# Macaron block: the hidden planes stored with the columns of the four token tiles by turns

## Chip, cores and metric

The kernel runs on one core of one Trainium2 chip. The metric is device time in microseconds of one execution, the median of several runs.

## The reference

What is computed is a block of two feed-forward layers with an attention layer between them, for 16 sequences of 512 tokens with 256 features:

```python
x = x + 0.5 * ffn(layernorm(x), w_gate, w_up, w_down)
x = x + attn(layernorm(x), wq, bq, wk, bk, wv, bv)      # one head of 256, rotary q and k
x = x + 0.5 * ffn(layernorm(x), w_gate, w_up, w_down)

def ffn(x, w_gate, w_up, w_down):                       # weights: int in -127..127, times 1/127
    gate, up = x @ wg.T, x @ wu.T                       # 256 -> 768
    return (silu(gate) * up) @ wd.T                     # 768 -> 256
```

## The kernel before, in words

The work is cut into 48 stages: 16 sequences through the first feed-forward, the 16 through attention, the 16 through the second feed-forward. Each stage holds one sequence, four tiles of 128 tokens. Stages overlap: layer statistics, normalization and the transposition of a later stage are issued between the steps of the current one, in an order written out by hand (`steady`, `opening`, and the main loops). There is no scheduler that would reorder it; each engine's queue is worked in the order of issue.

A feed-forward stage (`ffn`) takes six steps, one for each 128 of the 768 hidden features. One step `h` is:

- `products` (L339): eight matmuls of 512 columns. The stationary tile is a 128x128 piece of the gate or up weights, the moving operand is the stage's transposed, normalized input. That input is held as two planes, zT_h (rounded to float32r) and zT_l (the rest), which are multiplied one after the other and summed in PSUM. Within a plane the even and the odd columns lie apart, 1024 bytes from each other, and `some_columns` reads them by turns.
- `hidden`: ACT takes silu of the gate (L351, act), DVE multiplies with up (L353), into PSUM, tile "tr".
- `beside(h)`: pieces of other stages, of which zT_h (L217, on ACT) and zT_l (L222, on POOL) split the next stage's input into its planes.
- `hidden_planes`: through `planes`, ACT casts the product from PSUM to float32r, hT_h (L217), and DVE subtracts it from the product to get the rest, hT_l (L222). Both write a [128, 512] SBUF tile in the order token tile c, block a, column j, so that the 128 columns of token tile c lie side by side.
- `down` (L316): eight matmuls of 256 columns. For each plane and each token tile c the stationary tile is the 128x128 piece of hT_h or hT_l, the moving operand the down weights of this step, whose even and odd columns also lie 1024 bytes apart and are read by turns. They accumulate over the six steps in PSUM. After the sixth, `finish` (L289, DVE) adds them to x.

`down` is held back: step h's down projection is issued after the products of step h+2 (`LAG = 2`, the list `behind`). The last step of the last stage is done in two halves of two token tiles each (256 columns), so that its end comes sooner.

TensorE's weight load is an instruction of its own in the profile (PEld), one ahead of each matmul. Float32 matmuls of attention (L555, L586, L606, L625) show as two records each. Weights come in by DMA as integers and are cast on POOL in the prologue. A second, plain version of all layers stands behind a condition that the inputs of this reference don't meet.

Of the kernel before, what the change touches and what calls it, by code (L numbers as in the profile page):

```python
# [17 lines left out]
P = 128  # L18
Q = 32
NQ = P // Q  # L20
# [15 lines left out]
def macaron_kernel(ctx: ExitStack, tc: tile.TileContext, x, wq, wk, wv, bq, bk, bv, wg, wu, wd, cos, sin, out):  # L36
# [134 lines left out]
    def layers(exact, work, att):  # L171
# [35 lines left out]
        def planes(sources, pool, shape, name, bufs, engine, seen):  # L207


            if not exact:  # L210
                whole = pool.tile(shape, F32, name=f"{name}_w", tag=f"{name}_h", bufs=bufs)
                for n, source in enumerate(sources):
                    nc.scalar.copy(seen(whole, n), source)
                return [whole], lambda: None
            high = pool.tile(shape, F32R, name=f"{name}_h", tag=f"{name}_h", bufs=bufs)
            for n, source in enumerate(sources):
                nc.scalar.copy(seen(high, n), source)  # L217
            low = pool.tile(shape, F32R, name=f"{name}_l", tag=f"{name}_l", bufs=bufs)

            def rest():  # L220
                for n, source in enumerate(sources):
                    engine.tensor_tensor(seen(low, n), source, seen(high.bitcast(F32), n), ALU.subtract)  # L222

            return [high, low], rest
# [50 lines left out]
        def some_columns(t, tiles):  # L275

            some = slice(tiles.start * Q // 2, tiles.stop * Q // 2)
            return t.rearrange("p e (a f) -> p a f e", a=NQ)[:, :, some, :]

        def down_weights(h):  # L280

            if exact:
                return wf["d"][:, h // 2, :, h % 2, :].rearrange("p e f -> p f e")
            return wf["d"][:, h, :]

        def finish(i, half, acc, last):
            _, b = stages[i]
            x_half = xs[b][:, 2 * half : 2 * half + 2, :]
            nc.vector.scalar_tensor_tensor(x_half, acc, DOWN, x_half, ALU.mult, ALU.add)  # L289
            if last:  # L290
                queue = nc.scalar if i == len(stages) - 1 else nc.sync
                queue.dma_start(
                    out=out[b].rearrange("(p c) d -> p c d", c=NC)[:, 2 * half : 2 * half + 2, :], in_=x_half
                )
# [3 lines left out]
        def down_step(n):  # L298
            while len(behind) > n:
                behind.pop(0)()  # L300

        def ffn(i, last, beside):
            zT = ready.pop(i)
            accs = []

            def down(h, halves):

                if not accs:
                    accs.extend(ps_acc.tile([P, 2, D], F32, name="acc") for _ in range(NC // 2))


                for tiles_of in [range(NC)] if h < NH - 1 else [(0, 1), (2, 3)]:
                    for n in range(len(halves[0])):
                        for c in tiles_of:
                            t = halves[c // 2][n]
                            nc.tensor.matmul(  # L316
                                accs[c // 2][:, c % 2, :],
                                t[:, bass.ts(c % (t.shape[1] // P), P)],
                                down_weights(h),
                                start=h == 0 and n == 0 and c % 2 == 0,  # L320
                                stop=h == NH - 1 and n == len(halves[0]) - 1,
                                skip_group_check=True,
                            )
                    if h == NH - 1:
                        half = tiles_of[0] // 2
                        finish(i, half, accs[half], last)

            def products(hs, columns=slice(0, NC)):

                nt = columns.stop - columns.start  # L330
                pairs = [[ps_mm.tile([P, nt * P], F32, name="mm", tag="mm") for _ in "gu"] for _ in hs]
                if len(hs) > 1:

                    turns = [(0, 0, 0), (0, 0, 1), (0, 1, 0), (1, 0, 0), (1, 0, 1), (0, 1, 1), (1, 1, 0), (1, 1, 1)]
                    turns = [(turn, w) for turn in turns for w in range(2)]
                else:
                    turns = [((n, 0, k), w) for n in range(len(zT)) for w in range(2) for k in range(KD)]
                for (n, h, k), w in turns:
                    nc.tensor.matmul(  # L339
                        pairs[h][w],  # L340
                        wf["gu"[w]][:, k, bass.ts(hs[h], P)],
                        some_columns(zT[n][:, k], columns),
                        start=n == 0 and k == 0,
                        stop=n == len(zT) - 1 and k == KD - 1,
                    )
                return dict(zip(hs, pairs))

            def hidden(gate, up):

                act = work.tile(list(gate.shape), F32, name="act", tag="rope", bufs=6 if exact else 4)  # L350
                nc.scalar.activation(act, gate, AF.Silu, scale=WSCALE)  # L351
                hid = ps_tr.tile(list(gate.shape), F32, name="tr", tag="tr")
                nc.vector.tensor_tensor(hid, act, up, ALU.mult)  # L353
                return hid

            def hidden_planes(hid):
                tiles, rest = planes(
                    [hid.rearrange("p (a c j) -> p c a j", a=NQ, j=Q)],
                    work,
                    list(hid.shape),  # L360
                    "hT",
                    5,
                    nc.vector,
                    lambda t, _: t.rearrange("p (c a j) -> p c a j", a=NQ, j=Q),
                )
                rest()
                return tiles

            found = {}
            for h in range(NH):  # L370
                if last and i == len(stages) - 1 and h == NH - 1:
                    halves = [
                        hidden_planes(hidden(*products([h], slice(c, c + 2))[h])) for c in (0, 2)
                    ]
                    down_step(0)
                    down(h, halves)
                    break
                if h not in found:
                    found.update(products([0, 1] if exact and i == 0 and h == 0 else [h]))
                hid = hidden(*found.pop(h))  # L380
                down_step(LAG - 1)
                beside(h)
                tiles = hidden_planes(hid)
                behind.append(lambda h=h, tiles=tiles: down(h, [tiles] * 2))
                beside(h + 0.5)
# [268 lines left out]
        for b in range(B):  # L654
# [13 lines left out]
            if b + 1 < B:  # L668
                rotated = queries_keys(i + 1)

                def beside(a):
                    if a == 0:
                        measure(i + 3, (0, 1))
                    elif a == 2:
                        measure(i + 3, (2, 3))
# [75 lines left out]
```

## Time and profile before

| what | value |
|---|---|
| median of 3 runs | 907.65 us (907.25 to 908.27) |
| profiled execution, its own time | 907.49 us |
| its span, first to last instruction | 905.6 us |
| granted TensorE clock | 1.00 |
| matmuls of L316 | 1536, at a mean of 275 ns in the record |
| their weight loads | 1536, at a mean of 191 to 192 ns |
| hT_h on ACT, 512 columns | 191, mean 583 ns |
| hT_l on DVE, 512 columns | 191, mean 676 ns |

How to read the profile: a line gives engine, operation, what is written and from what, shapes, count, busy time and mean length. PE rows are matmuls, PEld rows weight loads. A matmul's record includes the way through the array, so records overlap: a record of 275 ns doesn't mean that 275 ns pass until the next one starts. For TensorE's pace one reads the starts. The chain of waits follows the work that ended last back in time; the table of stretches gives each engine's busy time in a part of the span.

### The profile page before, as it was taken

The page shows a single profiled execution, that of the slowest core. Times are in us where ns is not written, and L with a number is a line of the kernel's source. Part 1 is how long each engine was busy: PE and PEld are TensorE (multiplying, and loading weights), DVE is VectorE, ACT ScalarE, POOL GpSimd, SP SyncE. Part 2 cuts the span into 40 slices and gives each one's busy share as a digit, 9 for nine tenths or more (in the row PEclk, how much of TensorE's full clock was granted, in tenths as well). Part 3 has the DMA queues.
Part 4 walks back from the last instruction along what each step waited for, and adds up shares of the span by engine and source line. Part 5 has one row for each costly group of instructions (what it writes and reads, how often), then busy time and mean ns, then how long its engine had stood idle before and what let it go on. Part 6 is the DMA issues. An engine that isn't in the chain of part 4 may idle for free.

```text
span 905.6 us, 12799 instructions
## 1 busy us (share of the span) xinstructions
PE 897.8 (99%) x4392; PEld 711.0 (79%) x4392; DVE 675.3 (75%) x1392; ACT 405.4 (45%) x710; POOL 282.1 (31%) x536
## 2 busy tenths in 40 slices
PE   9999999999999999999999999999999999999997
PEld 7999999999975666666666666666899999999996
DVE  6887878777778777777777777777677778787765
ACT  5766666666631112222222222111566666666653
POOL 5342433333233333332222323333333323242310
PEclk9999999999999999999999999999999999999999
DMA  6424232221214444443433343344432223323211
GB/s 232 136 101 140 85 129 94 97 90 71 70 47 140 140 139 128 129 139 117 138 123 129 122 139 116 117 139 140 140 110 99 94 94 109 103 93 113 98 71 51
DMA packets 56042, 103.30 MB, mean 114 GB/s; under 512 B 6304, under 2 KB 33568, under 8 KB 53920
## 3 DMA queue, kind: packets, MB, share of 16 engines
q1 hardware_dynamic: 55392, 101.61, 33.7%
q8 instruction: 37, 0.61, 0.3%
q10 hardware_dynamic: 576, 0.79, 0.2%
q14 instruction: 37, 0.30, 0.1%
HBM read 53.09 MB, written 49.28 MB: 113 GB/s over the span
## 4 chain that ended last, share of the span: by engine, by line
PE 98%; DVE 0%; DMA 0%; ACT 0%; issue 0%; DVEq 0%
PE mm L339 37%; PE acc L316 19%; PE o_ps L625 12%; PE mm L555 12%; PE mm L606 12%; PE v_ps L586 6%; DMA x<-in_x_dram 0%; DVE st L122 0%; PE tr L165 0%; DVE x L289 0%; PE mm L165 0%; ACT zT_h L446 0%; DVE mv L124 0%; DVE z L505 0%; ACT rstd L127 0%
## 5 line engine op out<-in xcount | busy, mean ns | idle before, releaser
L353 DVE TENSOR_TENSOR tr<-act,mm 128x512 f32<-128x512 f32 (+1 forms) x193 | 133.6, 692 | 59.1 <-ACT act L351 55.1
L614 ACT ACTIVATE e<-mm,top 128x512 f32<-128x512 f32 x64 | 44.0, 688 | 294.0 <-DVE top L612 294.0
L222 DVE TENSOR_TENSOR hT_l<-tr,hT_h 128x512 fp32r<-128x512 f32 (+1 forms) x193 | 129.9, 673 | 54.9 <-ACT hT_h L217 53.6
L351 ACT ACTIVATE act<-mm 128x512 f32<-128x512 f32 (+1 forms) x193 | 115.4, 598 | 107.6 <-PE mm L339 105.0
L222 POOL TENSOR_TENSOR zT_l<-zT,zT_h 128x512 fp32r<-128x512 f32 x60 | 77.2, 1308 | 248.5 <-PE acc L316 208.1
L217 ACT CAST hT_h<-tr 128x512 fp32r<-128x512 f32 (+1 forms) x193 | 112.1, 581 | 83.6 <-DVE tr L353 83.1
L316 PEld LDWEIGHTS acc<-wd_r,hT_h 128*128 128x128 f32 x768 | 117.8, 191 | 10.5 <-issue 0.5
L316 PE MATMUL acc<-wd_r,hT_l 128*128 128x256 f32 x768 | 122.4, 275 | 0.0
L316 PE MATMUL acc<-wd_r,hT_h 128*128 128x256 f32 x768 | 122.2, 275 | 0.0
L339 PE MATMUL mm<-zT_h,wg_r 128*128 128x512 f32 (+1 forms) x386 | 116.2, 382 | 0.3 <-ACT zT_h L446 0.3
L339 PE MATMUL mm<-zT_l,wg_r 128*128 128x512 f32 (+1 forms) x386 | 114.7, 378 | 0.0
L339 PE MATMUL mm<-zT_l,wu_r 128*128 128x512 f32 (+1 forms) x386 | 114.7, 378 | 0.0
L339 PE MATMUL mm<-zT_h,wu_r 128*128 128x512 f32 (+1 forms) x386 | 114.7, 378 | 0.0
L625 PE MATMUL o_ps<-v,eT 128*128 128x257 f32 x512 | 113.9, 379 | 0.0
L606 PE MATMUL mm<-krot,qrot 128*128 128x512 f32 x256 | 112.8, 593 | 0.0
L625 PEld LDWEIGHTS o_ps<-v,eT 128*128 128x128 f32 x512 | 96.9, 189 | 14.7 <-issue 0.5
L316 PEld LDWEIGHTS acc<-wd_r,hT_l 128*128 128x128 f32 x768 | 103.8, 192 | 0.0
L150 ACT ACTIVATE z<-x,shift,rstd 128x256 f32<-128x256 f32 x190 | 101.1, 591 | 1.3 <-POOL shift L144 0.8
L568 POOL TENSOR_TENSOR qrot<-r0c,r1s 128x512 f32<-128x512 f32 x16 | 20.3, 1271 | 226.7 <-DVE r1s L561 226.7
L606 PEld LDWEIGHTS mm<-krot,qrot 128*128 128x128 f32 x256 | 48.3, 190 | 54.2 <-issue 52.4
L339 PEld LDWEIGHTS mm<-zT_l,wg_r 128*128 128x128 f32 x386 | 72.8, 189 | 10.3
L339 PEld LDWEIGHTS mm<-zT_l,wu_r 128*128 128x128 f32 x386 | 72.8, 189 | 10.2
(81 smaller groups left out, 1120.7 us busy)
## 6 DMA issues: line engine op xcount, KB each, us to landing
zT_d<-blocks SPq DMA_DIRECT2D x46, 512.0 KB, 2.6
zT<-zT_d SPq DMA_DIRECT2D x184, 128.0 KB, 2.8
eT_d<-eblocks SPq DMA_DIRECT2D x16, 1024.0 KB, 3.8
eT<-eT_d SPq DMA_DIRECT2D x64, 256.0 KB, 4.9
x<-in_x_dram SPq DMA_DIRECT2D x15, 512.0 KB, 4.5
out_dram<-x SPq DMA_DIRECT2D x30, 256.0 KB, 2.1
wg_i<-in_wg_dram SPq DMA_DIRECT2D x3, 256.0 KB, 4.2
wu_i<-in_wu_dram SPq DMA_DIRECT2D x3, 256.0 KB, 4.4
```

Source lines behind the costliest of these rows:

```text
L150: nc.scalar.activation(self.z[:, c, :], self.x[:, c, :], AF.Identity, bias=self.shift[:, c : c + 1], scale=self.rstd[:, c : c + 1],)
L217: nc.scalar.copy(seen(high, n), source)
L222: engine.tensor_tensor(seen(low, n), source, seen(high.bitcast(F32), n), ALU.subtract)
L316: nc.tensor.matmul(accs[c // 2][:, c % 2, :], t[:, bass.ts(c % (t.shape[1] // P), P)], down_weights(h), start=h == 0 and n == 0 and c % 2 ...
L339: nc.tensor.matmul(pairs[h][w], wf["gu"[w]][:, k, bass.ts(hs[h], P)], some_columns(zT[n][:, k], columns), start=n == 0 and k == 0, stop=n ...
L351: nc.scalar.activation(act, gate, AF.Silu, scale=WSCALE)
L353: nc.vector.tensor_tensor(hid, act, up, ALU.mult)
L555: nc.tensor.matmul(ps, w[:, k, t, :], zT[:, :, k, :], start=(k == 0), stop=(k == KD - 1))
L586: nc.tensor.matmul(ps, zT[:, a, k, :], wv_sb[:, k, :], start=(k == 0), stop=(k == KD - 1))
L606: nc.tensor.matmul(ps, q[:, t, bass.ts(a, P)], k[:, t, :], start=(t == 0), stop=(t == 1))
L614: nc.scalar.activation(e, ps, AF.Exp, bias=top, scale=1.0)
L625: nc.tensor.matmul(ps, eT[:, c, j, :], v[:, j, :], start=(j == 0), stop=(j == NC - 1))
```

## The change

The tiles of the hidden planes get the shape [128 features, 128 columns, 4 token tiles] in place of [128, 512]. What lay at column c x 128 + p now lies at column p x 4 + c. ACT's cast and DVE's subtraction write in that new order (and DVE reads hT_h in it), from the same PSUM tile read in the same order as before. The stationary operand of L316 becomes 128 columns with a step of 4 words of 4 bytes. In the last step's halves there are two token tiles, and the step is 2 words. Values, number of instructions, their order, buffers and semaphores are the same; lines behind L356 move down by two.

```diff
@@ down(), L316
-                                t[:, bass.ts(c % (t.shape[1] // P), P)],
+                                t[:, :, c % t.shape[2]],
                                 down_weights(h),
@@ hidden_planes()
             def hidden_planes(hid):
+
+                nt = hid.shape[1] // P
                 tiles, rest = planes(
                     [hid.rearrange("p (a c j) -> p c a j", a=NQ, j=Q)],
                     work,
-                    list(hid.shape),
+                    [P, P, nt],
                     "hT",
                     5,
                     nc.vector,
-                    lambda t, _: t.rearrange("p (c a j) -> p c a j", a=NQ, j=Q),
+                    lambda t, _: t.rearrange("p (a j) c -> p c a j", a=NQ),
                 )
                 rest()
                 return tiles
```

## Prediction

> **What bounds the kernel now.** I read the page's first part and its chain before anything else: which engine is full, and which one the chain that ended last runs through.
>
> ```profile
> PE 897.8 (99%) x4392; PEld 711.0 (79%) x4392; DVE 675.3 (75%) x1392; ACT 405.4 (45%) x710; POOL 282.1 (31%) x536
> ...
> PE 98%; DVE 0%; DMA 0%; ACT 0%; issue 0%; DVEq 0%
> PE mm L339 37%; PE acc L316 19%; PE o_ps L625 12%; PE mm L555 12%; PE mm L606 12%; PE v_ps L586 6%; DMA x<-in_x_dram 0%; DVE st L122 0%; PE tr L165 0%; DVE x L289 0%; PE mm L165 0%; ACT zT_h L446 0%; DVE mv L124 0%; DVE z L505 0%; ACT rstd L127 0%
> ```
>
> TensorE sets the end. Time is won or lost only where its matmuls come closer or further apart. The change touches the 1536 matmuls of L316, 19% of the chain. A busy PE is not PE at its peak, so next I read the order in time of the weight loads (PEld) and the matmuls (PE) around one down projection: start, length, what, how many.
>
> ```profile
> 151.07 0.61 PE L316 MATMUL acc<-wd_r,hT_h 128*128 128x256 f32 x4
> 151.41 0.53 PEld L316 LDWEIGHTS acc<-wd_r,hT_l 128*128 128x128 f32 x4
> ...
> 151.52 0.61 PE L316 MATMUL acc<-wd_r,hT_l 128*128 128x256 f32 x4
> 151.86 0.30 PEld L339 LDWEIGHTS mm<-zT_h,wg_r 128*128 128x128 f32 x2
> 151.97 0.60 PE L339 MATMUL mm<-zT_h,wg_r 128*128 128x512 f32 x2
> ...
> 152.19 0.41 PEld L339 LDWEIGHTS mm<-zT_h,wu_r 128*128 128x128 f32 x2
> ...
> 152.40 0.59 PE L339 MATMUL mm<-zT_h,wu_r 128*128 128x512 f32 x2
> ```
>
> From 151.07 to 151.97 lie eight down matmuls: 0.90 us / 8 = 112 ns each. Two gate/up matmuls, twice as wide, take 0.43 us: 215 ns each. The single starts in the trace say more. Gate/up starts lie 215 or 216 ns apart. Down starts lie 109 or 110 ns apart after the first of a step and 111 or 112 after nearly all others. The weight load of the next matmul starts 2 or 3 ns after each matmul's start, and the next matmul starts 107 to 109 ns after that. So in the down projection **the load of the stationary tile fills the whole interval**; beside a gate/up matmul half of the interval is spare. By these rows a load can get shorter and win only 2 to 3 ns, down to the 109 that 256 columns take; whatever makes it longer is paid in full.
>
> **What the change removes, adds and moves.** The instructions of each engine stay the same in number and order: 1536 down matmuls with their loads, 193 casts hT_h on ACT, 193 subtractions hT_l on DVE. No wait, no DMA and no buffer is added; no queue is reordered. Only addresses change, in three places:
>
> 1. The loads of L316 read 128 columns at a step of 4 words (16 bytes) where they read 128 neighbours. In the two half-width pieces of the last stage the step is 8 bytes.
> 2. ACT writes hT_h (L217) at that step.
> 3. DVE reads hT_h and writes hT_l (L222) at that step.
>
> **Part 1, the load.** No load in this trace has a step, so I bound it. These are the loads of L316, with smallest, median and largest length in ns:
>
> ```profile
> L316 PEld LDWEIGHTS acc<-wd_r,hT_h x768: 189/192/192, 13.7 to 899.1; 128*128 128x128 f32 x192
> ...
> L316 PEld LDWEIGHTS acc<-wd_r,hT_l x768: 192/192/192, 14.3 to 899.3; 128*128 128x128 f32 x192
> ```
>
> Those of the prologue's idle matmuls, in the same columns:
>
> ```profile
> L482 PEld LDWEIGHTS mm<-still x14: 188/330/333, 1.4 to 8.0; 128*128 128x128 f32 x14
> ```
>
> And, from the groups by form, those of the second block's transposes (busy us, mean ns):
>
> ```profile
> L165 PEld LDWEIGHTS mm<-ident,z 128*128 128x128 f32 x8 | 0.9, 142 | 0.0
> ```
>
> A load of one column (L664) takes 80 ns, so 128 columns cost some 109 more. A transpose's load is 47 to 50 shorter, so the memory can deliver contiguous columns faster; and in the first microseconds, when the 512-column matmuls come 426 ns apart instead of 216, the load takes 330. The pace of the load thus follows the array, not the memory, which speaks for no change with the address. If a step did make it shorter, the gain would end at 109 ns: in the trace 1347 down matmuls and 16 narrow gate/up ones sit at 111.6 on average (x 2.4 = 3.3 us), and the first gate matmul of each step, 182 of them, at 218.6 instead of 215.7 (0.5 us). The lower end is -3.8 us.
>
> Above: the nearest rows of stepped SBUF reading are ACT's zT_h and POOL's zT_l, which read zT at 8 bytes.
>
> ```profile
> L217 ACT CAST hT_h<-tr x193: 372/586/629, 12.3 to 898.2; 128x512 fp32r<-128x512 f32 x191, 128x256 fp32r<-128x256 f32 x2
> ...
> L217 ACT CAST zT_h<-zT x60: 652/834/895, 35.9 to 871.5; 128x512 fp32r<-128x512 f32 x60
> ```
>
> ACT needs 652 to 895 where the same cast from PSUM needs 586: a factor of 1.11 to 1.53. POOL needs 1309 where contiguous inputs (L568) need 1271: 1.03. On 107 ns of reading the factor 1.53 is 56 ns, times 1536 = +87 us; 1.11 is +18 us; 1.03 is +5 us. Against these rows stands one of TensorE's own ports: the moving operand of L339 already jumps 1024 bytes at every column (the e-planes) and still delivers 512 columns in 216 ns, one jump per 0.42 ns; the load would jump once per 0.83 ns. I take **0**: it is TensorE's row, and the load's pace is the array's. Both ends stay for the range.
>
> One rule of the Trainium skill speaks against the change: "SBUF — State Buffer", section "Specifications (TRN2)", says that SBUF has lines of 16 bytes, that at least two hits per line are needed for full bandwidth, and that each step to a new line costs. At 16 bytes every column would be its own line. Estimated from that page as half the pace, each load would be 107 ns longer, 164 us in all, and the time 1072. The trace differs for the moving operand, which changes line at every column at full pace; no run here shows it for a load.
>
> **Parts 2 and 3, ACT and DVE.** Neither is on the chain; the question is how much cover they have. First the busy time in one stage of the second feed-forward (PE, PEld, DVE, ACT, POOL), then DVE's order in time there.
>
> ```profile
> 698.80:714.50 15.70, 15.70 (x97) 14.43 (x96) 12.09 (x25) 10.18 (x19) 5.03 (x10) 1.00 0.29 102
> ```
>
> ```profile
> 692.86 0.70 DVE L353 TENSOR_TENSOR tr<-act,mm 128x512 f32<-128x512 f32 x1 [0.48 <-ACT act L351]
> 694.32 0.69 DVE L222 TENSOR_TENSOR hT_l<-tr,hT_h 128x512 fp32r<-128x512 f32 x1 [0.75 <-ACT hT_h L217]
> 695.49 0.70 DVE L353 TENSOR_TENSOR tr<-act,mm 128x512 f32<-128x512 f32 x1 [0.48 <-ACT act L351]
> ```
>
> A stage has six steps of 2.62 us. In five of them DVE waits 0.48 us for act, whose ACT instruction itself waits for the matmuls: 2.4 us of true slack per stage. The 0.75 before hT_l is ACT's latency; a longer cast lengthens it unless other DVE work lies there (three of six steps). hT is wanted late: the down projection of step h is queued behind the products of h+1 and h+2, some 5.3 us after the last product of h, and the chain act, tr, hT_h, hT_l ends after 2.8.
>
> The price of the write: at least 0 (the contiguous forms go at one element per 0.82 ns on ACT and 0.98 on DVE, from the 512- and 256-wide rows, and no address makes that shorter); DVE's L448, with a PSUM input at 8 bytes, takes 682, no more than hT_l's 691. From above, zT_h's 0.07 to 0.31 us; as an estimate, twice the time per element: 0.42 on ACT, 0.50 on DVE. At zT_h's median (834 - 586 = 0.25 on both) a stage asks 6 x 0.25 + 3 x 0.25 = 2.25 us of the 2.4: still hidden. I take that, and count **0**. At the upper estimate it is 6 x 0.50 + 3 x 0.42 = 4.3, less 2.4 = 1.9 us per stage, times 32 = +60 us. The tail has little cover: the last hT_l ends at 899.04 and its load starts at 899.23, so a few tenths of a us could show there; I leave that in the range.
>
> **Sum.** 0 + 0 + 0 against the profiled execution's own 907.49 us (span 905.6 and 1.9 around it), which lies 0.16 below the median of the runs, 907.65. Forecast 907.5.
>
> **The rivals.**
>
> - *The load becomes shorter.* For it: it fills the interval now, and any reading conflict that it suffers from contiguous columns would be gone; in the prologue two contiguous matmuls of 256 columns start 118 ns apart, where stepped ones take 109 to 112. Against: its pace follows the array. 907.5 - 3.8 = 903.7.
> - *The load becomes longer* (the slower side). Place: L316; price: 1.54 us for every ns per load; it decides from the first ns on, 1.2 ns being 0.2%. For it: the load has no slack at all, and ACT's stepped reads of SBUF get longer while other engines work (652 alone, 772 to 895 beside DVE and POOL). Against: the moving operand's row. 912 to 994 by the factors above, near 950 in the middle.
> - *DVE becomes the bound.* Its price above 0.4 us per step (with ACT's half) comes through: from 908 to 968. For it: 77% busy in these stages. Against: L448.
> - *Nothing reaches TensorE* is the forecast itself, and also the case that the change doesn't do what it is meant to.
>
> **How the numbers follow.** Nothing reaches TensorE: 0.33. Shorter load: 0.24, faster by 0.4%. Longer load: 0.24. DVE the bound: 0.15. Small collisions of the stepped writes with TensorE's reads, 2 to 10 us: 0.04. This kernel's measurement can tell about 0.2% (1.8 us) from no change. Faster 0.24, same 0.33, slower 0.24 + 0.15 + 0.04 = 0.43. The range begins below the full gain, at 903, and goes up to 985: it leaves out the longer loads near and beyond their upper bound (about 0.13) and the odd mishap. The likeliest case's own range is 906 to 909.
>
> **What would show it.** Loads of L316 at 192 ns and down starts 112 apart: the forecast. Loads near 189 and starts at 109: the first rival. Longer loads, and a PEld that is no longer idle ahead of L316's matmuls: the second. PE idle ahead of L316 or L339 with DVE or ACT as releaser, hT_l above 1.1 us: the third. I would be wrong at the root if TensorE's load reads another way than its moving port.

## The result, and the profile after

The changed kernel takes 1077.61 us (median of 4 runs, 1077.27 to 1077.93) where the kernel before takes 907.45 beside it (4 runs, 907.17 to 908.27): a ratio of 1.187, 95% interval 1.186 to 1.189. That is 170 us slower, and outside the predicted range.

The page of the changed kernel: busy time of the engines, and the chain of work that ended last with its shares by engine and by line.

```profile
PE 1065.9 (99%) x4392; PEld 882.7 (82%) x4392; DVE 781.4 (73%) x1392; ACT 557.5 (52%) x710; POOL 281.6 (26%) x536
...
PE 97%; DVE 1%; ACT 1%; issue 0%; DMA 0%; DVEq 0%
PE acc L316 31%; PE mm L339 30%; PE o_ps L627 10%; PE mm L557 10%; PE mm L608 10%; PE v_ps L588 5%; ACT hT_h L217 1%; DVE tr L353 0%; DVE st L122 0%; DMA x<-in_x_dram 0%; DVE hT_l L222 0%; PE tr L165 0%; DVE x L289 0%; DVE zT_l L450 0%; DVE mv L124 0%
```

TensorE still sets the end, and its share of busy time is still 99%: that number says nothing of the loss. The chain does: L316 had 19% of 905.6 us and now has 31% of 1075.4. Busy time grew on PE, PEld, DVE and ACT, with the counts unchanged: the same instructions, longer.

The weight loads of L316, smallest, median and largest length in ns:

```profile
L316 PEld LDWEIGHTS acc<-wd_r,hT_h x768: 197/329/335, 13.7 to 1068.9; 128*128 128x128 f32 x192
...
L316 PEld LDWEIGHTS acc<-wd_r,hT_l x768: 197/331/334, 14.9 to 1069.2; 128*128 128x128 f32 x192
```

330 where it was 192. The starts of the matmuls tell what that costs; TensorE in order of time (start, length, what, how many), around one down projection:

```profile
171.57 0.99 PE L316 MATMUL acc<-wd_r,hT_h 128*128 128x256 f32 x4
...
172.40 1.10 PE L316 MATMUL acc<-wd_r,hT_l 128*128 128x256 f32 x4
...
173.33 0.60 PE L339 MATMUL mm<-zT_h,wg_r 128*128 128x512 f32 x2
```

Eight down matmuls take 173.33 - 171.57 = 1.76 us, where they took 0.90. In the single starts the first interval of a step is 124 ns (the step's first load already runs beside the last gate/up matmul, from 171.36 us on) and the other seven are 233, against 112 before. 124 + 7 x 233 = 1755 ns, 865 more than the 890 or so before; times 192 steps that is 166 us. Summed over the whole trace, the time from each L316 start to the next matmul's start went from 171.3 to 339.5 us: 168.2 of the 169.8 us by which the profiled span grew (905.6 to 1075.4). The rest is a few short waits.

The two instructions that write the tile, in the same columns as the loads above:

```profile
L217 ACT CAST hT_h<-tr x193: 424/1536/1562, 12.0 to 1066.8; 128x512 fp32r<-128x512 f32 x191, 128x256 fp32r<-128x256 f32 x2
L222 DVE TENSOR_TENSOR hT_l<-tr,hT_h x193: 445/1275/1487, 13.6 to 1067.3; 128x512 fp32r<-128x512 f32 x191, 128x256 fp32r<-128x256 f32 x2
```

ACT's cast went from 586 to 1536, DVE's subtraction from 691 to 1275. DVE's order in time in the second feed-forward, with the wait ahead of each instruction in brackets:

```profile
790.43 0.74 DVE L353 TENSOR_TENSOR tr<-act,mm 128x512 f32<-128x512 f32 x1
792.77 1.25 DVE L222 TENSOR_TENSOR hT_l<-tr,hT_h 128x512 fp32r<-128x512 f32 x1 [1.60 <-ACT hT_h L217]
793.92 0.69 DVE L353 TENSOR_TENSOR tr<-act,mm 128x512 f32<-128x512 f32 x1
```

tr no longer waits for act, and so no longer for TensorE: DVE waits for ACT's cast, and ACT's cast waits for tr. tr, hT_h, hT_l and the next tr follow one another in a loop, 793.92 - 790.43 = 3.49 us long. TensorE's step has also become 3.49 us (2.62 before). So two things grew at once and by nearly the same amount, and the trace of the change alone can't say which of them costs the 170 us.

### The profile page after: what moved, and what is told of

Same layout as the page of the kernel before. It is cut to its first block, busy times and chain, and to the rows that moved or that the text cites. A ratio compares the mean times of both kernels' runs of the same rounds, so it can differ in the third digit from the quotient of the medians.

```text
span 1075.4 us, 12799 instructions
## 1 busy us (share of the span) xinstructions
PE 1065.9 (99%) x4392; PEld 882.7 (82%) x4392; DVE 781.4 (73%) x1392; ACT 557.5 (52%) x710; POOL 281.6 (26%) x536
## 4 chain that ended last, share of the span: by engine, by line
PE 97%; DVE 1%; ACT 1%; issue 0%; DMA 0%; DVEq 0%
PE acc L316 31%; PE mm L339 30%; PE o_ps L627 10%; PE mm L557 10%; PE mm L608 10%; PE v_ps L588 5%; ACT hT_h L217 1%; DVE tr L353 0%; DVE st L122 0%; DMA x<-in_x_dram 0%; DVE hT_l L222 0%; PE tr L165 0%; DVE x L289 0%; DVE zT_l L450 0%; DVE mv L124 0%
## 5 line engine op out<-in xcount | busy, mean ns | idle before, releaser
L217 ACT CAST hT_h<-tr 128x512 fp32r<-128x512 f32 (+1 forms) x193 | 285.7, 1480 | 191.3 <-DVE tr L353 191.2
L222 DVE TENSOR_TENSOR hT_l<-tr,hT_h 128x512 fp32r<-128x512 f32 (+1 forms) x193 | 247.4, 1282 | 174.3 <-ACT hT_h L217 174.2
L316 PE MATMUL acc<-wd_r,hT_l 128*128 128x256 f32 x768 | 215.6, 397 | 0.0
L316 PEld LDWEIGHTS acc<-wd_r,hT_h 128*128 128x128 f32 x768 | 197.0, 323 | 6.8 <-issue 1.9
L316 PEld LDWEIGHTS acc<-wd_r,hT_l 128*128 128x128 f32 x768 | 200.5, 330 | 0.2 <-DVE hT_l L222 0.2
L316 PE MATMUL acc<-wd_r,hT_h 128*128 128x256 f32 x768 | 196.9, 372 | 0.0
L353 DVE TENSOR_TENSOR tr<-act,mm 128x512 f32<-128x512 f32 (+1 forms) x193 | 136.6, 708 | 2.1 <-ACT act L351 2.1
L351 ACT ACTIVATE act<-mm 128x512 f32<-128x512 f32 (+1 forms) x193 | 126.4, 655 | 15.7 <-PE mm L339 15.7
L339 PE MATMUL mm<-zT_h,wg_r 128*128 128x512 f32 (+1 forms) x386 | 116.3, 382 | 0.5 <-ACT zT_h L448 0.3
L339 PE MATMUL mm<-zT_h,wu_r 128*128 128x512 f32 (+1 forms) x386 | 114.9, 379 | 0.7 <-DVE tr L353 0.7
L339 PE MATMUL mm<-zT_l,wu_r 128*128 128x512 f32 (+1 forms) x386 | 114.9, 379 | 0.0
L339 PE MATMUL mm<-zT_l,wg_r 128*128 128x512 f32 (+1 forms) x386 | 114.8, 378 | 0.0
L339 PEld LDWEIGHTS mm<-zT_h,wu_r 128*128 128x128 f32 x386 | 72.7, 189 | 11.2 <-DVE tr L353 1.1
L339 PEld LDWEIGHTS mm<-zT_l,wu_r 128*128 128x128 f32 x386 | 73.0, 190 | 10.2
L339 PEld LDWEIGHTS mm<-zT_l,wg_r 128*128 128x128 f32 x386 | 72.9, 189 | 10.1
```

What stands on the lines that cost most here:

```text
L316: nc.tensor.matmul(accs[c // 2][:, c % 2, :], t[:, :, c % t.shape[2]], down_weights(h), start=h == 0 and n == 0 and c % 2 == 0, stop=h == ...
L339: nc.tensor.matmul(pairs[h][w], wf["gu"[w]][:, k, bass.ts(hs[h], P)], some_columns(zT[n][:, k], columns), start=n == 0 and k == 0, stop=n ...
```

## The experiments

The theories at the outset. **Load**: the load of the stationary tile at a step of 16 bytes takes 233 ns, and that alone is the loss. **Writers**: the stepped writes of ACT and DVE make a loop that TensorE waits for. **Sum**: each has a part of it. Beside these runs the kernel before took 907.8 to 908.1 us (medians). The two reordered kernels of 953 and 935 us were timed five times, every other run below once. Repeated executions of one kernel lie within about 1.5 us here, so a difference of that size between single runs says nothing. Where an expectation names another run: e1 is the reading alone, e2 the writing alone, e4 the down matmuls dealt between the gate/up matmuls, e10 ACT alone. The first group parts the theories, the second asks what about the step costs, the third looks for cover, the fourth parts ACT from DVE.

### The reading alone

The tiles are written as before; only the stationary operand of L316 is read at a step of 4 words (so the columns that it multiplies are others than the reference's).

```diff
-                                t[:, bass.ts(c % (t.shape[1] // P), P)],
+                                t.rearrange("p (m c) -> p m c", m=P)[:, :, c % (t.shape[1] // P)],
```

> Only the loads of L316 read at a step of 16 bytes; ACT and DVE write neighbours as before. The tokens that meet in one stationary tile are others than the reference's, so the output's rows are exchanged. Theory 'load' (a stepped load takes about twice as long and TensorE pays it): 1070 to 1077 us, loads near 330 ns, down starts 233 ns apart. Theory 'writes' (the stepped writes on ACT and DVE set the pace): 907 to 915 us.

Measured: 1074.43 us, 167 over before and 3.2 under the change. The page's groups (count, busy us, mean ns of one, idle time ahead of them and what ended it):

```profile
PE 1063.0 (99%) x4392; PEld 881.4 (82%) x4392; DVE 678.7 (63%) x1392; ACT 400.3 (37%) x710; POOL 281.1 (26%) x536
...
L316 PEld LDWEIGHTS acc<-wd_r,hT_l 128*128 128x128 f32 x768 | 200.4, 329 | 0.0
...
L222 DVE TENSOR_TENSOR hT_l<-tr,hT_h 128x512 fp32r<-128x512 f32 (+1 forms) x193 | 129.5, 671 | 53.9 <-ACT hT_h L217 53.7
...
L217 ACT CAST hT_h<-tr 128x512 fp32r<-128x512 f32 (+1 forms) x193 | 111.7, 579 | 82.1 <-DVE tr L353 82.1
```

ACT and DVE are as fast as before (579 and 671 on average), and the loss is there all the same: loads 329, starts 124 and then 233. The reading suffices.

### The writing alone

The changed tiles and writes, but the stationary operand is taken from neighbouring columns (other columns than the reference's).

```diff
-                                t[:, :, c % t.shape[2]],
+                                t.rearrange("p m c -> p (m c)")[:, bass.ts(c % t.shape[2], P)],
```

> Only ACT and DVE write (and DVE reads hT_h) at a step of 16 bytes; the loads of L316 read 128 neighbours, so that tokens are mixed between tiles and the output's rows are exchanged. Theory 'load': below 1000 us, and 907 to 915 if the writes shrink to what they need undisturbed. Theory 'writes': 1070 to 1077 us. A third: both bound separately, since tr 0.70 + hT_h 1.1 to 1.5 + hT_l 1.28 is 3.1 to 3.5 us in the loop between ACT and DVE where TensorE before needs 2.62 a step: 192 x 0.45 to 0.87 = 990 to 1075 us here too, although e1 is as slow as the change.

Measured: 1067.08 us, 159 over before, with loads at 192 again. The page, in the same columns, with the chain that ended last:

```profile
PE 957.9 (90%) x4392; PEld 730.0 (69%) x4392; DVE 791.9 (74%) x1392; ACT 530.9 (50%) x710; POOL 281.0 (26%) x536
...
PE 45%; ACT 21%; issue 17%; DVE 16%; DMA 0%; ACTq 0%; DVEq 0%
...
L222 DVE TENSOR_TENSOR hT_l<-tr,hT_h 128x512 fp32r<-128x512 f32 (+1 forms) x193 | 255.2, 1322 | 154.3 <-ACT hT_h L217 153.8
L217 ACT CAST hT_h<-tr 128x512 fp32r<-128x512 f32 (+1 forms) x193 | 266.6, 1381 | 202.2 <-DVE tr L353 202.2
...
L316 PE MATMUL acc<-wd_r,hT_l 128*128 128x256 f32 x768 | 133.4, 291 | 31.3 <-DVE hT_l L222 31.1
```

Here TensorE waits for DVE, and no engine is full: the chain runs through ACT and DVE by turns. DVE in order of time shows why:

```profile
785.78 0.71 DVE L353 TENSOR_TENSOR tr<-act,mm 128x512 f32<-128x512 f32 x1
788.09 1.22 DVE L222 TENSOR_TENSOR hT_l<-tr,hT_h 128x512 fp32r<-128x512 f32 x1 [1.60 <-ACT hT_h L217]
789.21 0.70 DVE L353 TENSOR_TENSOR tr<-act,mm 128x512 f32<-128x512 f32 x1
791.53 1.17 DVE L222 TENSOR_TENSOR hT_l<-tr,hT_h 128x512 fp32r<-128x512 f32 x1 [1.61 <-ACT hT_h L217]
```

tr, then ACT's cast (DVE waits), then hT_l, then the next tr: at the medians 0.70 + 1.48 + 1.29 = 3.47 us a step. 159.3 us over 192 steps is 0.83, and 2.62 + 0.83 = 3.45. Neither ACT (50% busy) nor DVE (74%) is the bound by its busy time; their loop is. (TensorE's granted clock averages 0.975 in this run, and 0.958 in that of ACT alone below, with stretches of 3.4 us at 0.50; in the others it is 0.998 or more. The three instructions of the loop give the step without it. What the slow stretches show about ACT comes under "ACT alone, DVE alone".)

So each half alone costs nearly the whole: 167 and 159, together 170. The larger of the two counts, not their sum (908 + 167 + 159 would be 1234). **Sum** falls. In the change the load sets the pace, and the writers' loop lies beside it with nothing to spare.

### Other steps of the stationary operand

What about 16 bytes costs: the step as such, or the number of 16-byte lines touched? Three runs, each with the kernel before and only the read of L316 changed: a step of 8 bytes, of 12 bytes, and of 20 bytes. The 20 bytes don't fit into the tile, so that run reads the gate weights as its stationary operand. In all three the columns multiplied aren't the reference's.

```diff
-                                t[:, bass.ts(c % (t.shape[1] // P), P)],
+ 8 bytes:                       t.rearrange("p (m s) -> p m s", s=2)[:, bass.ts(c // 2, P), c % 2],
+ 12 bytes:                      t[:, : 3 * P].rearrange("p (m s) -> p m s", s=3)[:, :, c % 3],
+ 20 bytes:                      wf["g"].rearrange("p k h -> p (k h)")[:, c : c + 5 * (P - 1) + 1 : 5],
```

> Only the loads of L316 read at a step, of 8 bytes (64 lines of 16 bytes for 128 columns); writes as before, the output's rows exchanged. Theory 'a new 16-byte line costs': two columns share a line, so a load stays near 110 to 120 ns and the time between 908 and 925 us (the change's last stage, at 8 bytes, shows starts 117 to 123 ns apart). Theory 'any step costs': near 1074 us.

> Only the loads read at a step, of 12 bytes (96 lines for 128 columns); output's rows exchanged. If each line costs 233 / 128 = 1.8 ns: 96 x 1.8 = 175 ns a start, 1536 x 63 = +97, about 1004 us. If full price begins above 8 bytes: 1074. If it begins at 16: 908 to 925.

> Only the loads read at a step, of 20 bytes, and from the gate weights in place of the hidden planes (whose tile is too short for it), so the down projection multiplies other numbers. Every column is its own line as at 16 bytes, but successive columns move by one word within it. Theory 'line': 1074 us as e1. Theory 'the same place in each line' (16 bytes special): 908 to 930.

Measured: 918.46, 994.21 and 1062.10 us. The loads of L316, smallest, median and largest ns; first at 8 bytes:

```profile
L316 PEld LDWEIGHTS acc<-wd_r,hT_l x768: 192/198/201, 14.1 to 909.4; 128*128 128x128 f32 x192
```

at 12 bytes:

```profile
L316 PEld LDWEIGHTS acc<-wd_r,hT_l x768: 192/263/268, 14.7 to 986.3; 128*128 128x128 f32 x192
```

at 20 bytes:

```profile
L316 PEld LDWEIGHTS acc<-wd_r,wg_r x1536: 294/319/325, 13.6 to 1053.4; 128*128 128x128 f32 x192
```

| step | lines of 16 bytes that 128 columns touch | ns between starts, the first interval of a step left out |
|---|---|---|
| 4 bytes (before) | 32 | 112 |
| 8 | 64 | 117 to 123 |
| 12 | 96 | 172 to 181 |
| 16 | 128 | 233 |
| 20 | 128 | 220 to 231 |

From 64 lines on the interval is about 1.8 ns for each line (64 x 1.82 = 117, 96 x 1.82 = 175, 128 x 1.82 = 233); below that, the 109 to 112 of the columns themselves. A step beyond a line costs no more than one of a line, so lines count, not distance. Two columns to a line are nearly free (7 ns a load), one is not. This agrees with the page "SBUF — State Buffer" of the Trainium skill, section "Specifications (TRN2)" (lines of 16 bytes, two hits per line for full bandwidth): the prediction cited that rule, estimated 1072 us from it, and let the moving operand overrule it.

### The moving operand

The prediction held that TensorE's moving operand jumps at every column and loses nothing. Two runs test that on the matmuls of L339, with nothing of the change: one reads the 512 columns of zT at a step of 16 bytes, the other reads moving columns one after another in L339 and L316, with no planes by turns. Both multiply columns in another order than the reference's.

```diff
             t = ...                      # some_columns, for all four token tiles
+            if tiles == slice(0, NC):
+ step 16:       return t.rearrange("p e (f s) -> p s e f", s=4)
+ neighbours:    return t.rearrange("p e f -> p (e f)")       # and down_weights without its rearrange
```

> The moving operand of L339 is read at a step of 16 bytes (four runs of 128) in place of two planes by turns; stationary tiles as before; the output's rows are exchanged. If the moving port pays per line like the load: 512 columns in 430 to 930 ns in place of 216, so 1240 us or more. If the moving port has no such price, as the prediction concluded from the planes: 907.5. Between them: a price that the planes avoid because each line is used four times within eight columns.

> The moving operands of L339 and L316 are read neighbour by neighbour, without the turns between planes; rows and columns of the output are exchanged. If alternating planes buy nothing: 907.5. If two columns of one line in a row cost the moving port something (two matmuls of 256 neighbouring columns in the prologue start 118 ns apart, and 109 to 112 with planes): 512 columns in 216 to 233 ns, 256 in 112 to 120, up to 1536 x 17 + 1536 x 8 = +38 us.

Measured: 1283.76 us at 16 bytes, 946.11 with neighbours. TensorE in order of time, first at 16 bytes, two matmuls to a line:

```profile
200.54 1.08 PE L341 MATMUL mm<-zT_h,wg_r 128*128 128x512 f32 x2
201.44 1.10 PE L341 MATMUL mm<-zT_h,wu_r 128*128 128x512 f32 x2
202.36 1.10 PE L341 MATMUL mm<-zT_l,wg_r 128*128 128x512 f32 x2
```

The starts of pairs lie 0.90 to 0.92 us apart: 460 ns a matmul, against 216 before. And with neighbours:

```profile
200.14 0.62 PE L341 MATMUL mm<-zT_h,wu_r 128*128 128x512 f32 x2
200.60 0.63 PE L341 MATMUL mm<-zT_l,wg_r 128*128 128x512 f32 x2
```

0.46 us, 230 a matmul. So the moving port pays for new lines too: 0.90 ns a column where each column has a line of its own. Two planes by turns are not such a case. A jump of 1024 bytes comes at every column, but the even plane's line is back two columns later, and each line serves four of eight columns. The prediction counted jumps, where, by these runs, uses of a line had to be counted. That the port keeps both lines at hand is a guess that fits; no run reads two planes with a new line at every column. Planes by turns even beat neighbours: a matmul of 512 columns takes 216 ns on average with planes and 233 with neighbours, one of 256 takes 112 and 119. That makes 38 us in all, the upper end of what was expected. The count of lines doesn't give this, and no run here explains it.

### Cover for the loads

The prediction also held that beside a gate/up matmul half of the interval is spare. If so, down matmuls dealt singly between gate/up matmuls would hide a long load, or give the 2.4 ns of the rival "shorter load". First the kernel before with each down matmul issued after one of the eight products (`products` takes one step of the `down` due after each of its matmuls; `finish` moves behind `hidden`), then the same with the stepped reading of the first experiment.

```diff
-                found.update(products([0, 1] if exact and i == 0 and h == 0 else [h]))
+                steps = behind.pop(0)() if len(behind) >= LAG else iter(())
+                pairs, ends = products([0, 1] if exact and i == 0 and h == 0 else [h], steps=steps)
...
+                    ends = next(steps, ends)        # in products, after each matmul
```

> The kernel before, with the eight down matmuls of a step issued by turns with the eight gate/up matmuls of the step two later, in place of behind them. Same loads, same addresses. If a load fills the interval of a 256-column matmul, the 512-column one beside it covers it, and down starts are set by the columns: 3.8 us less, 903.7 us. If 112 ns is the matmul's own pace: no change, 907.5. If the later end of the products delays act and hT: above 908.

> e1 (stepped loads alone, output rows exchanged) with the order of e4. If loads follow one another and only their sum counts against the columns: a pair needs 109 + 231 + 5 = 345 ns in place of 216 + 112 = 328, 1536 x 17 ns = +26 us, about 934 us. If a stepped load holds up TensorE whatever lies beside it: as e1, 1070 to 1077.

Measured, without the step: 953.39 us, ratio 1.050 (1.049 to 1.052). TensorE in order of time, at the seam of two stages:

```profile
150.05 0.38 PE L349 MATMUL mm<-zT_h,wg_r 128*128 128x512 f32 x1
151.65 0.35 PE L324 MATMUL acc<-wd_r,hT_h 128*128 128x256 f32 x1 [1.21 <-DVE x L289]
151.83 0.38 PE L349 MATMUL mm<-zT_h,wg_r 128*128 128x512 f32 x1
152.05 0.27 PE L324 MATMUL acc<-wd_r,hT_h 128*128 128x256 f32 x1
152.16 0.38 PE L349 MATMUL mm<-zT_h,wu_r 128*128 128x512 f32 x1
```

A down and a gate/up matmul take 109 + 218.5 = 327.5 ns here, and 111.6 + 216 = 327.6 apart from each other: the 2.4 ns moves to the neighbour and is not to be won in this way. The 46 us are something else, the wait in the second line: the first down matmul of a stage needs `finish` of the stage before, which this order issues too late. There are 31 such stalls, nearly all of 1.60 us from start to start in place of 0.22; together they are 42 of the 46 us. (The trace puts 25 of them down to `finish`, 6 to ACT's hT_h.)

With the step: 986.79 us, 33.4 over its partner (26 were expected for the loads), where the same reading costs 167 in the old order. A pair takes 128 + 218 = 346 ns, near the two loads one after the other (233 + 112 = 345), and not the 327 of the columns. By this run loads don't overlap each other: a long one can borrow the spare time of a short one's interval, and their sum counts where it is more than the columns take. No other mixture was run.

As a last try for the 2.4 ns, the same without mixing in the first two steps of a stage, to keep the stall away:

```diff
-                steps = behind.pop(0)() if len(behind) >= LAG else iter(())
+                steps = behind.pop(0)() if len(behind) >= LAG and h >= LAG else iter(())
```

> As e4, but the down projections that end a stage stay behind the products, so that the sums are added to x as early as in the kernel before; 4 of 6 steps are by turns. In e4 a pair of starts took 109 + 218.5 ns where apart they take 111.6 + 216: if that is so here, the 2.4 ns per load are a fixed price of the pair, no cover wins them, and the time is 907 to 909 us. If a covered load wins them: 907.5 - 2/3 x 3.8 = 905.0 us.

Measured: 934.84 us, ratio 1.030 (1.028 to 1.031); pairs again at 109 + 218. A stall remains in each stage, shorter:

```profile
713.98 0.38 PE L349 MATMUL mm<-zT_h,wg_r 128*128 128x512 f32 x1
...
714.92 0.35 PE L324 MATMUL acc<-wd_r,hT_h 128*128 128x256 f32 x1 [0.56 <-DVE x L289]
```

From the gate matmul to the down matmul 0.94 us pass instead of 0.22; 31 such stalls, nearly all of that length, are 23 of the 27 us. No version faster than the kernel before was found.

### ACT alone, DVE alone

Which of the two writers makes the loop long? In the first run only ACT writes hT_h at the step (DVE then reads it at the step, and writes neighbours); in the second only DVE writes hT_l at the step, and hT_h is written and read as before. L316 reads neighbours in both, so the first run's columns aren't the reference's.

```diff
 ACT alone, planes():
+                    put = seen if name != "hT" else (lambda t, _: ...)          # the old order of columns
-                    engine.tensor_tensor(seen(low, n), source, seen(high.bitcast(F32), n), ALU.subtract)
+                    engine.tensor_tensor(put(low, n), source, seen(high.bitcast(F32), n), ALU.subtract)
 DVE alone:
-                nc.scalar.copy(seen(high, n), source)
+                nc.scalar.copy(put(high, n), source)
-                    engine.tensor_tensor(seen(low, n), source, seen(high.bitcast(F32), n), ALU.subtract)
+                    engine.tensor_tensor(seen(low, n), source, put(high.bitcast(F32), n), ALU.subtract)
```

> Only hT_h is written at a step of 16 bytes (and read so by DVE); hT_l is written to neighbours and all loads read neighbours, so tokens are mixed in the low plane against the high one and the output is another. If DVE's reading costs as much as its writing, hT_l stays at 1.28 us and the loop tr 0.70 + hT_h 1.5 + hT_l 1.28 gives e2's 1067 us. If the writing alone costs DVE, hT_l returns to 0.69: 2.9 us a step against 2.62, 192 x 0.3 = +55, about 960 us.

> Only hT_l is written at a step of 16 bytes by DVE; hT_h and all loads go to and read neighbours; the output is another, as in e10. If DVE's writing costs: hT_l 1.28, loop 0.70 + 0.59 + 1.28 = 2.57 a step, just under TensorE's 2.62: 907 to 930 us. If it was DVE's reading: hT_l 0.69 and 907.5.

Measured: 1064.75 us for ACT alone, with hT_h at 1456; 963.55 for DVE alone, with hT_h at 585. hT_l (smallest, median, largest ns) where only its reading is stepped:

```profile
L223 DVE TENSOR_TENSOR hT_l<-tr,hT_h x193: 425/1301/1561, 14.2 to 1055.1; 128x512 fp32r<-128x512 f32 x191, 128x256 fp32r<-128x256 f32 x2
```

and where only its writing is:

```profile
L224 DVE TENSOR_TENSOR hT_l<-tr,hT_h x193: 439/1456/1645, 13.1 to 954.7; 128x512 fp32r<-128x512 f32 x191, 128x256 fp32r<-128x256 f32 x2
```

DVE pays for reading at 16 bytes (1301), for writing (1456), and for both at once no more than for one (1275). ACT's stepped write makes two instructions long, its own and the subtraction that reads its result: 0.70 + 1.46 + 1.30 = 3.46 us a loop, against (1064.75 - 908.1) / 192 + 2.62 = 3.44. It is nearly the whole loss of the writing.

The writing of hT_l alone adds 55 us, more than the 22 at most that were expected, because hT_l takes 1456 ns and not 1280, and tr 829 (median) where it took about 700. The same loop then has 0.83 + 0.59 + 1.46 = 2.88 us, against (963.55 - 908.1) / 192 + 2.62 = 2.91. DVE itself is nearly full there: it is busy for 92 of the 100 us from 700 to 800 us, where it was 78 in the kernel before.

What sets the length of ACT's stepped write? The slow stretches of the clock in the runs of the writing alone and of ACT alone give a hint. First a cast in such a stretch (granted clock 0.50), from the writing alone, then one at full clock from the same run:

```profile
985.24 1.09 ACT L217 CAST hT_h<-tr 128x512 fp32r<-128x512 f32 x1 [1.65 <-DVE tr L353]
985.26 1.06 PE L339 MATMUL mm<-zT_l,wg_r 128*128 128x512 f32 x2
...
986.11 1.06 PE L339 MATMUL mm<-zT_l,wu_r 128*128 128x512 f32 x2
```

```profile
789.95 1.54 ACT L217 CAST hT_h<-tr 128x512 fp32r<-128x512 f32 x1 [0.49 <-DVE tr L353]
...
790.35 0.59 PE L339 MATMUL mm<-zT_h,wu_r 128*128 128x512 f32 x2
...
790.78 0.59 PE L339 MATMUL mm<-zT_l,wg_r 128*128 128x512 f32 x2
```

Beside gate/up matmuls that start 427 ns apart (two in 0.85 us) the cast takes 1.09 us, beside those 215 apart 1.54. This holds throughout: in the change and these two runs, 129 casts lie wholly beside gate/up matmuls 215 to 220 ns apart and take 1512 to 1569 ns; 39 lie wholly beside gate/up matmuls in a stretch at clock 0.50 and take 1085 to 1097. The unstepped casts of the kernel before take 567 to 629 beside gate/up matmuls at full pace. DVE's hT_l goes the same way in the same two runs: 1511 to 1629 ns for the 37 wholly beside the faster ones, 1079 to 1089 for the 9 beside the slower. So a stepped write by ACT costs some 0.5 us beside TensorE at half pace, and nearly as much again at full pace. No run changed TensorE's pace alone; this is read from the traces and not tested, and by which way the two meet isn't shown.

## Why the prediction was wrong

- **The bound** was read rightly. "The load of the stationary tile fills the whole interval" and "whatever makes it longer is paid in full": the load's interval grew by 121 ns on seven of eight matmuls, and 168.2 of the 169.8 us by which the span grew lie between L316's starts. The reading alone shows it (1074.43).
- **Part 1 is the step that failed**: "I take **0**: it is TensorE's row, and the load's pace is the array's." The row was the right engine's but not the right case's: the moving operand's planes use each line four times in eight columns, the changed load uses each line once. Where the moving operand is given the changed load's pattern, it takes 460 ns in place of 216. The interval of 109 to 112 is a floor that holds at 32 lines; from 64 lines on (119 on average) the lines set the pace, at some 1.8 ns each.
- **The upper end of part 1** (+87 us) failed for the same reason. Its rows, ACT's and POOL's reads at 8 bytes, have two columns to a line; on the load itself 8 bytes cost 7 ns each (918.46), 16 bytes 121. A bound from a row at another step was no bound. Only the estimate from the page's rule, 1072 us, came near; that a new line at each column would halve the pace was a choice that came out well (121 ns on seven of eight loads, for 107 on each). No row that the prediction used had one column to a line, and where that is so the range has to stay open above.
- **Parts 2 and 3**: "still hidden", counted 0. In the change they are hidden, but only since the load became as slow; alone they cost 159 us. The upper estimates, +0.42 us on ACT and +0.50 on DVE, were too small above all for ACT: +0.95 and +0.58 were measured. L448, which spoke for no cost, has an 8-byte step, and that on a PSUM input. The slack was counted by DVE's idle time per stage; the loop through both engines (0.70 + 0.59 + 0.69 = 1.98 before, of 2.62) is what had to be compared with the step.
- **The rival "longer load"** named the mechanism, the place and the point from which it decides (the first ns). Its price was mis-sized, 3 to 56 ns for the 121 measured.
- **The rival "DVE becomes the bound"** also came true, in the writing alone: 1067 us instead of at most 968, with DVE and ACT in one loop rather than DVE full. Where DVE alone writes at the step it is nearly full (92%), at 963.55 us.
- **The rival "shorter load"** fell: the load got longer, and where it is covered the 2.4 ns go to the next interval (327.5 for 327.6).
- **The sign that was named**, "I would be wrong at the root if TensorE's load reads another way than its moving port": it was wrong at the root, though not because the load alone pays: both lose time where each column has a line of its own (1.8 and 0.90 ns a column). The moving operand as it stands doesn't read in that way.

Open: why ACT's stepped write (1456 to 1536 ns at the median) goes with TensorE's pace beside it, and why planes by turns are read faster than neighbours.

## What to carry to other kernels

Ahead of a change of layout, count for every operand that it touches, stationary, moving, ACT's and DVE's, reads and writes, how often a 16-byte line is used while it is at hand; a jump at every column can be free (two planes by turns) and a small step can double the time (one fp32 to a line). A row bounds the cost of an operation only if its lines are used in the same way; a row at 8 bytes says nothing of 16. When two stages grow together, undo each alone before adding their costs: here each cost nearly the whole, since the slower of two loops sets the pace, and a loop through two engines can bind while neither is full.

## What was not expected of the hardware

- Interval of the load by its step: 112, 119, 176, 233 and 225 ns on average at 4, 8, 12, 16 and 20 bytes, some 1.8 ns a line from 64 lines on; the moving operand pays 0.90 ns a line, half of that.
- Moving columns from two planes by turns come faster (216 ns for 512) than neighbours (228 to 241, 233 on average).
- A long load takes spare time from the interval of a short one: 346 ns for a pair, against 345 for two loads in a row (one run).
- DVE at one fp32 to a line is slow by reading as by writing, and both together cost no more than one (1301, 1456, and 1275 to 1293, from 691).
- ACT's write at one fp32 to a line takes 1512 to 1569 ns beside gate/up matmuls at full pace and 1085 to 1097 beside those at half the pace, for 586 to neighbours.
- The two halves of the last step, at 8 bytes, cost little: ACT 424 and 437 ns (372 and 382 before), DVE 445 and 451 (424 before).
